# Two planned costs of a list-scheduled transformer kernel: the norm's application on GpSimd, and the engine of the first layer's key copies

## The chip, the cores and the metric

One core of a Trainium2 chip runs the whole program. The time is device microseconds for one execution, from launch to end. The kernel before the change was timed three times: 2121.66, 2126.34 and 2129.11 us, so the median is 2126.34 us. The engines are named as in the profile: PE is the matrix engine, PEld its weight loads, DVE the vector engine, ACT the scalar engine, POOL is GpSimd and SP the engine that only issues transfers.

## What is computed

Four transformer layers run over 16 sequences of 256 rows with 128 features. Each layer is a norm and an attention, then a norm and a feed-forward block, each added to the running `x`. All of it is 32-bit floating point.

```python
x = x + _L0_attn_ref(_layernorm(x), gamma, w_q, w_kv, null_kv, q_scale, k_scale, w_out)
x = x + _L0_ffn_ref(_layernorm(x), w1, b1, w2, b2)
x = x + _L1_attn_ref(...); x = x + _L1_ffn_ref(...)
x = x + _L2_attn_ref(...); x = x + _L2_ffn_ref(...)      # eight experts, the best one per row
x = x + _L3_attn_ref(...); x = x + _L3_ffn_ref(...)

def _layernorm(x, eps=1e-05):
    m = jnp.mean(x, -1, keepdims=True); v = jnp.var(x, -1, keepdims=True)
    return (x - m) / jnp.sqrt(v + eps)

# layer 0 attention, 16 heads of 64
q = _l2norm(q) * q_scale
k = _l2norm(k) * k_scale
sim = einsum('bhid,bhjd->bhij', q, k) * 8.0 + dist * slopes      # causal, two null keys
out = softmax(sim) @ v @ w_out
```

## The kernel before

**An order written by a planner.** The kernel does not issue instructions where its code stands. Each piece of work is a call `step(eng, p, ns, emit, r, w, m)`: the engine, a rank `p` that says how early the step is wanted, a planned length `ns`, a function that issues the instructions, and the tiles that it reads, writes or changes. When all steps are known, `Plan.run` goes through an imagined time line. Each engine has a time from which it is free; a step is ready when the steps it depends on have ended, plus a fixed delay for a signal to be seen (`SEEN`, for example 60 ns on DVE and 110 ns on POOL). Among the steps that an engine could start within 40 ns of its earliest, the one with the lowest rank is taken. Then the engine whose pick starts earliest goes first, its `emit` is called, and its free time moves on by the planned length. The result is a fixed order of instructions in each engine's queue. On the chip each queue runs strictly in that order, and waits where a tile isn't ready. So a planned length never delays an instruction by itself: it only decides which order, which engine and which buffer the steps get.

**Steps with two engines.** `"AD"` stands for ACT or DVE, `"DP"` for DVE or POOL, with one planned length for each. Such a step stands in both engines' lists and goes to the one that can start it first in the plan; the planned end breaks ties. A step of the kind `"AD"` counts on DVE with its rank raised by 8 (`SHY`), so DVE takes it only where it has nothing more urgent.

**The norm** (`layernorm`, line 456) is three steps: `stats` on DVE (four instructions, lines 464 and 465), `scale` on POOL (variance plus epsilon, line 469 or 471, and the power −½, line 436), and `apply`, two instructions of 128x128 in line 477 that subtract the mean and multiply. In the first layer `apply` is called with `eng="DVE"`; in all later places (attention and feed-forward of layer 1, attention and expert gate of layer 2, attention and feed-forward of layer 3) with the default `"DP"`, 96 norms in all. The step before the change is planned with 520 ns on DVE and 620 ns on POOL. What reads its result is the turn (transposition) in PE, line 432, by way of `turned` and `in_halves`.

**The first layer's preparation** (`prep0`, line 787) projects `xn` to raw queries and keys (line 404), copies them out of the accumulation banks (`evac`, lines 448 on ACT and 450 on DVE), squares and sums them (lines 812 and 813), takes the power −½ on POOL (line 436, planned with 2892 ns), and in `scaled` (line 821) multiplies the raw values in place on DVE (line 827), turns them on PE (line 432) into two banks, one for each half, and copies each half into `Q` or `K`. The two copies of a query turn are `evac` steps, free to go to ACT or DVE. The two copies of a key turn, line 843, also multiply by a per-partition scale `kqs` and are fixed to ACT, planned with 570 ns. There are 32 key turns and so 64 such copies, 128x512 each. The scores' matmuls (line 404, tiles `K` and `Q`) read them, then line 866 (DVE) and line 874 (ACT) make the softmax's numerators, and line 534 (POOL) divides.

**Banks.** All matrix results go through eight accumulation banks, `t0x` to `t7x`; a bank is free again when its last copy has been made. In the first layer each queue holds work of two or three sequences at once, since the preparation of a sequence runs up to 26 ranks ahead of its scores and a sequence takes 16 ranks.

The parts that set which engine gets a step, in `Plan.run`:

```python
could.append((t, s.p + (self.SHY if e == "DVE" and s.eng[0] == "ACT" else 0), s.no, s))
...
t, p, _, s = min((c for c in could if c[0] <= soon + 40), key=lambda c: c[1:3])
pick = (t, t + s.ns[e] if len(s.eng) > 1 else t, p, e, s)
if best is None or pick[:3] < best[:3]:
    best = pick
```

Of the kernel before, what the change touches and what calls it, by code (L numbers as in the profile page):

```python
# [11 lines left out]
AF = mybir.ActivationFunctionType  # L12
ALU = mybir.AluOpType
# [54 lines left out]
class Plan:  # L68
# [27 lines left out]
    def step(self, eng, p, ns, emit, r=(), w=(), m=(), mode=None, tail=None):  # L96
        s = Step()
        s.eng = {"AD": ("ACT", "DVE"), "DP": ("DVE", "POOL")}.get(eng, (eng,))
        s.ns = dict(zip(s.eng, ns)) if len(s.eng) > 1 else {eng: ns}
        s.p, s.emit, s.mode, s.tail, s.no = p, emit, mode, tail, len(self.steps)  # L100
        val = lambda x: x if isinstance(x, Value) else self.key(x)
        r, w, m = ([val(x) for x in xs] for xs in (r, w, m))
        deps = {}
        for v in r:
            deps.update((id(d), d) for d in v.writers)
        for v in w:
            deps.update((id(d), d) for d in v.readers)
        for v in m:
            deps.update((id(d), d) for d in v.writers + v.readers)
        for v in r:  # L110
            v.readers.append(s)
        for v in w:
            v.writers.append(s)
        for v in m:
            v.writers, v.readers = [s], []
        s.touch = list({id(v): v for v in r + w + m if v.home}.values())
        for v in s.touch:
            v.steps += 1

        for src in r:  # L120
            if src.home in self.BANKS:
                for made in src.writers:
                    for v in w:
                        if v.home and v not in made.touch:
                            made.touch.append(v)
                            v.steps += 1
        deps.pop(id(s), None)
        s.deps, s.left, s.users, s.end = list(deps.values()), len(deps), [], None
        for d in s.deps:
            d.users.append(s)  # L130
        self.steps.append(s)
        return s
# [107 lines left out]
def preln_d4_kernel(ctx: ExitStack, tc: tile.TileContext, x_in, vecs, rows, nullk, nullv,  # L240
                    wa0, wlat, wb1, wa2, wex, gatew, wa3, out):
    nc = tc.nc
    PSUM = bass.MemoryType.PSUM
    plan = Plan()
    step, get = plan.step, plan.get
# [195 lines left out]
    X = [plan.key(f"x{b}") for b in range(B)]  # L441
# [14 lines left out]
    def layernorm(b, p, xn, at, times=1, behind=(), eng="DP"):  # L456

        ln, x = get("ln"), x_of(b)  # L460

        def stats(e):
            for i in range(2):
                nc.vector.bn_stats(ln.t[0][:, i, :], x[:, i, :])
                nc.vector.bn_aggr(ln.t[1][:, i, :], ln.t[0][:, i, :])  # L465

        def scale(e):
            if times == 1:
                nc.gpsimd.tensor_scalar(ln.t[2], ln.t[1][:, :, 1], LN_EPS, 1.0, ALU.add, ALU.mult)  # L469
            else:  # L470
                nc.gpsimd.tensor_scalar(ln.t[2], ln.t[1][:, :, 1], 1.0 + LN_EPS, LN_EPS * LN_EPS, ALU.mult, ALU.add)
            rsqrt(ln.t[2], 2)

        def apply(e):
            for i in range(2):
                v = nc.vector if e == "DVE" else nc.gpsimd
                v.tensor_scalar(xn.t[:, (at + i) * D:(at + i + 1) * D], x[:, i, :], ln.t[1][:, i, 0:1],
                                ln.t[2][:, i:i + 1], ALU.subtract, ALU.mult)

        step("DVE", p, 788, stats, r=[X[b]], w=[ln])  # L480
        step("POOL", p, 1070, scale, m=[ln])
        step(eng, p, (520, 620) if eng == "DP" else 520 if eng == "DVE" else 620, apply, r=[X[b], ln] + list(behind), w=[xn])

    def turned(p, xn, nt, gamma=None):

# [265 lines left out]
    kqs = cp.tile([P, 1], F32, tag="kqs", name="kqs")  # L751
# [12 lines left out]
    def null2(e):  # L764
# [7 lines left out]
         r=["nss"], w=[nk_ps], mode="P")  # L772
    step("DVE", -13, 100, lambda e: nc.vector.scalar_tensor_tensor(
        nkT, nk_ps.t[:, 0:16].rearrange("p (c n) -> p c n", n=2), kqs, steepT.unsqueeze(2).broadcast_to([P, 8, 2]), ALU.mult, ALU.mult),
         r=[nk_ps, "steepT"], w=["nkT"])
# [11 lines left out]
    def prep0(b):  # L787
        st = {}
        lo, hi = first[0, b - 1] if b else A0 - 16, first[0, b] - 2
        lo = max(lo, hi - LEAD0)  # L790
        order = ("x p00 p01 p20 p21 p10 p11 p30 t00 p31 t01 v0 v1 t10 v2 v3 t11").split()
        at = {what: lo + 2 + (hi - lo - 2) * i / len(order) for i, what in enumerate(order)}
        xn = get("r")
        layernorm(b, lo, xn, 0, times=2, eng="DVE")
        xnT = turned(at["x"], xn, 2, gamma=vec("gamma"))
        st.update(Q=[get("Q"), get("Q")], K=[get("K"), get("K")], V=[get("V"), get("V")], pn=get("pn"))
        for c in range(2):
            step("POOL", at["t10"] - 4, 180,
                 lambda e, c=c: nc.gpsimd.tensor_copy(st["K"][c].t[:, :, 0:2], nkT[:, 4 * c:4 * c + 4, :]),
                 r=["nkT"], w=[st["K"][c]])  # L800
        raws, ss = {}, [get("ss") for _ in range(4)]

        def project(n, c):

            i, which = divmod(n, 2)
            p = at[f"p{n}{c}"]
            ps, sq = get("t"), get("sq")
            raw = raws[n, c] = get("r")
            step("PE", p, 862, lambda e: mm(ps.t, xnT.t[:, i * P:(i + 1) * P], wqkv[:, (2 * which + c) * 512:(2 * which + c + 1) * 512]),
                 r=[xnT, f"wA.{2 * which + c}"], w=[ps], mode="P")  # L810
            evac(p, raw, ps, lambda: (raw.t, ps.t))
            step("ACT", p, 520, lambda e: nc.scalar.activation(sq.t, raw.t, AF.Square), r=[raw], w=[sq])
            step("DVE", p, 592, lambda e: nc.vector.tensor_reduce(ss[n].t[:, c * 8:(c + 1) * 8], sq.t.rearrange("p (h d) -> p h d", d=64),
                                                                  AX.X, ALU.add), r=[sq], w=[ss[n]])
            if c == 1:
                step("DVE", p, 80, lambda e: nc.vector.tensor_scalar(ss[n].t, ss[n].t, 1e-24, None, ALU.max), m=[ss[n]])  # L816
                step("POOL", p - 6, 2892, lambda e: rsqrt(ss[n].t, 16), m=[ss[n]])
                if which == 1:
                    step("DVE", p - 6, 80, lambda e: nc.vector.tensor_tensor(ss[n].t, ss[n].t, steep, ALU.mult), r=["steep"], m=[ss[n]])

        def scaled(which, c):

            p, t, of = at[f"t{which}{c}"], [get("t"), get("t")], [raws[which, c], raws[2 + which, c]]
            for i in range(2):
                n, raw = 2 * i + which, of[i]
                r = lambda raw=raw: raw.t.rearrange("p (h d) -> p h d", d=64)
                step("DVE", p - 2, 598, lambda e, n=n, r=r: nc.vector.tensor_tensor(
                    r(), r(), ss[n].t[:, c * 8:(c + 1) * 8].unsqueeze(2).broadcast_to([P, 8, 64]), ALU.mult), r=[ss[n]], m=[raw])

            def turn(e):  # L830
                for i in range(2):
                    for k in range(4):
                        turned_halves(t, i * 256 + k * 64, of[i].t[:, k * P:(k + 1) * P])

            step("PE", p, 500, turn, r=of, w=t, mode="S")
            for z in range(2):
                src = lambda z=z: t[z].t.rearrange("p (i c q) -> p c i q", i=2, c=4)
                dst = lambda z=z, x=st["KQ"[which == 0]][c], a=2 * which: x.t[:, :, a:a + 256].rearrange(
                    "p c (i z q) -> p c i z q", i=2, z=2)[:, :, :, z]
                if which == 0:  # L840
                    evac(p, st["Q"][c], t[z], lambda src=src, dst=dst: (dst(), src()))
                else:
                    step("ACT", p - 8, 570, lambda e, src=src, dst=dst: nc.scalar.activation(dst(), src(), AF.Copy, scale=kqs),
                         r=[t[z]], w=[st["K"][c]])

        def values(k):
            i, c = divmod(k, 2)
            ps, p = get("t"), at[f"v{k}"]
            step("PE", p, 862, lambda e: mm(ps.t, xnT.t[:, i * P:(i + 1) * P], wqkv[:, 2048 + c * 512:2048 + (c + 1) * 512]),
                 r=[xnT, f"wA.{4 + c}"], w=[ps], mode="P")  # L850
            evac(p, st["V"][i], ps, lambda: (st["V"][i].t[:, c * 512:(c + 1) * 512], ps.t))

        for n in (0, 2, 1, 3):
            for c in range(2):
                project(n, c)
        for which in range(2):
            for c in range(2):
                scaled(which, c)
        for k in range(4):
            values(k)  # L860
        return st
# [60 lines left out]
    for b in range(B):  # L922
        st = prep0(b)
# [139 lines left out]
    for b in range(B):  # L1063
        st = prep1(b)
# [302 lines left out]
    for b in range(B):  # L1367
        st = prep2(b)
# [123 lines left out]
    for b in range(B):  # L1492
        st = prep3(b)
# [95 lines left out]
```

## Time and profile before

| what | value |
|---|---|
| median of three runs | 2126.34 us |
| the profiled execution, whole / its span | 2132.18 us / 2130.5 us |
| granted clock of PE, mean | 0.982 |
| busy of the span: PE, PEld, DVE | 2030.3, 1395.8, 1636.7 us |
| busy of the span: ACT, POOL | 1660.5, 1159.3 us |
| line 843 on ACT, 128x512 | 64 instructions, 677 to 707 ns |
| line 477 on POOL, 128x128 | 134 instructions, 779 to 817 ns |
| line 477 on DVE, 128x128 | 122 instructions, 309 to 976 ns, median 342 ns |
| copies of 128x512 into `Q` (first layer) | 32 on ACT, median 612 ns; 32 on DVE, median 679 ns |

The span runs from the first to the last instruction; the whole time has 1.7 us more around it. The busy time of an engine is the union of its instructions; PE's is close to the span throughout, while the other three have between 470 and 971 us in which nothing runs. In time order the program does layer 0 up to some 577 us, layer 1 to about 1100 us, layer 2's attention to about 1740 us, with the experts and layer 3 mixed at the end.

The 64 key copies lie between 30.7 and 565.9 us. The norms that may go to either engine begin at about 577 us: 67 of the 96 went to POOL, 29 to DVE.

### The profile page before, as it was taken

How to read it: one execution, taken by the hardware profiler on the slowest of the kernel's cores; microseconds unless marked ns; L12 is line 12 of the kernel's file. 1: busy time of each engine (PE TensorE's matmuls, PEld its weight loads, DVE VectorE, ACT ScalarE, POOL GpSimd, SP SyncE). 2: the span in 40 equal slices, each digit the busy share in tenths (PEclk: the TensorE clock that was granted, in tenths of full speed). 3: DMA queues.
4: the chain of work that ended last, by engine and by line, in shares of the span. 5: the costliest groups of instructions: out<-in, count | busy, mean ns of one | idle time of the engine just before them, and what ended most of it. 6: DMA issues, size and time to landing. Idle time of an engine off the chain costs nothing.

```text
span 2130.5 us, 86226 instructions
## 1 busy us (share of the span) xinstructions
PE 2030.3 (95%) x34860; PEld 1395.8 (66%) x34860; DVE 1636.7 (77%) x6393; ACT 1660.5 (78%) x4834; POOL 1159.3 (54%) x2157
## 2 busy tenths in 40 slices
PE   7999999999999999999999999999999998998997
PEld 4667777777665444544546677777887775775665
DVE  7999999999887766667665467777676778677997
ACT  6999999998887776767766668877666778677996
POOL 7888888898842121212223346666454974227642
PEclk9999999999999999999999999999999998998999
DMA  5000000000140000000000000000442001441000
GB/s 168 2 2 2 2 2 2 2 2 3 32 61 12 2 3 3 3 3 3 3 3 1 2 4 5 7 7 18 123 122 74 22 7 45 140 146 29 15 8 18
DMA packets 60303, 59.08 MB, mean 28 GB/s; under 512 B 28016, under 2 KB 49024, under 8 KB 59904
## 3 DMA queue, kind: packets, MB, share of 16 engines
q1 hardware_dynamic: 57680, 49.33, 8.3%
q8 instruction: 274, 4.49, 0.9%
q0 software_dynamic: 2048, 4.20, 0.6%
q14 instruction: 125, 1.02, 0.2%
q10 hardware_dynamic: 176, 0.03, 0.0%
HBM read 43.32 MB, written 10.22 MB: 25 GB/s over the span
## 4 chain that ended last, share of the span: by engine, by line
PE 73%; DVE 12%; POOL 7%; ACT 6%; issue 3%; another core or an unknown queue 0%; POOLq 0%; ACTq 0%; DVEq 0%
PE t0x L404 9%; PE t4x L404 9%; PE t6x L404 8%; PE t1x L404 8%; PE t7x L404 8%; PE t3x L404 7%; PE t2x L404 7%; PE t5x L404 7%; PE t1x L432 1%; PE t5x L432 1%; PE t6x L432 1%; PE t7x L432 1%; PE t0x L432 1%; PE t4x L432 1%; PE t2x L432 1%
## 5 line engine op out<-in xcount | busy, mean ns | idle before, releaser
L469 POOL TENSOR_SCALAR ln_rs4x<-ln_mv4x 128x2 f32<-128x2 f32 x24 | 4.6, 193 | 92.1 <-DVE ln_mv4x L465 91.1
L469 POOL TENSOR_SCALAR ln_rs2x<-ln_mv2x 128x2 f32<-128x2 f32 x21 | 4.7, 224 | 82.7 <-DVE ln_mv2x L465 81.9
L469 POOL TENSOR_SCALAR ln_rs0x<-ln_mv0x 128x2 f32<-128x2 f32 x21 | 4.1, 193 | 78.1 <-DVE ln_mv0x L465 70.6
L469 POOL TENSOR_SCALAR ln_rs3x<-ln_mv3x 128x2 f32<-128x2 f32 x23 | 4.8, 210 | 70.9 <-DVE ln_mv3x L465 64.1
L502 POOL TENSOR_TENSOR x<-x,row_sb 128x256 f32<-128x256 f32 x48 | 35.0, 730 | 6.2 <-DVE row_sb L1118 3.4
L436 POOL TENSOR_TENSOR ss0x<-ss0x,mhalf 128x16 f32<-128x16 f32 x11 | 31.9, 2902 | 8.5 <-DVE ss0x L816 7.3
L469 POOL TENSOR_SCALAR ln_rs1x<-ln_mv1x 128x2 f32<-128x2 f32 x23 | 4.4, 193 | 57.0 <-DVE ln_mv1x L465 55.9
L534 POOL TENSOR_SCALAR probs4x<-probs4x,sums2x 128x256 f32<-128x256 f32 (+2 forms) x44 | 20.4, 477 | 25.3 <-PE t5x L404 16.5
L534 POOL TENSOR_SCALAR probs0x<-probs0x,sums2x 128x256 f32<-128x256 f32 (+2 forms) x40 | 19.2, 493 | 26.3 <-DVE sums2x L529 16.0
L534 POOL TENSOR_SCALAR probs0x<-probs0x,sums4x 128x256 f32<-128x256 f32 (+2 forms) x44 | 21.7, 506 | 21.2 <-DVE sums4x L529 20.9
L436 POOL TENSOR_TENSOR ss3x<-ss3x,mhalf 128x16 f32<-128x16 f32 x11 | 32.9, 2992 | 0.1
L436 POOL TENSOR_TENSOR ss1x<-ss1x,mhalf 128x16 f32<-128x16 f32 x11 | 32.8, 2986 | 0.1
L436 POOL TENSOR_TENSOR ss2x<-ss2x,mhalf 128x16 f32<-128x16 f32 x11 | 31.9, 2901 | 0.9 <-DVE sums1x L529 0.9
L436 POOL TENSOR_TENSOR ss5x<-ss5x,mhalf 128x16 f32<-128x16 f32 x10 | 30.5, 3045 | 0.2
L436 POOL TENSOR_TENSOR ss4x<-ss4x,mhalf 128x16 f32<-128x16 f32 x10 | 29.4, 2944 | 0.5 <-DVE sums1x L529 0.5
L1060 POOL TENSOR_TENSOR x<-x,sq0x 128x512 f32<-128x512 f32 x4 | 5.1, 1275 | 44.9 <-DVE sq0x L1058 44.9
L534 POOL TENSOR_SCALAR probs2x<-probs2x,sums0x 128x256 f32<-128x256 f32 (+2 forms) x44 | 19.7, 463 | 17.8 <-DVE sums1x L529 14.0
L534 POOL TENSOR_SCALAR probs2x<-probs2x,sums4x 128x256 f32<-128x256 f32 (+2 forms) x40 | 20.9, 535 | 12.3 <-DVE sums4x L529 11.9
L534 POOL TENSOR_SCALAR probs3x<-probs3x,sums3x 128x256 f32<-128x256 f32 (+2 forms) x44 | 19.8, 464 | 13.4 <-DVE sums3x L529 12.1
L621 DVE CUSTOM_DVE_ANT_0 probs2x<-t6x,mask 128x128 f32<-128x128 f32 (+1 forms) x44 | 11.9, 323 | 19.6 <-PE t2x L404 7.6
L534 POOL TENSOR_SCALAR probs5x<-probs5x,sums3x 128x256 f32<-128x256 f32 (+2 forms) x44 | 20.5, 482 | 11.9 <-DVE sums3x L529 11.8
L534 POOL TENSOR_SCALAR probs0x<-probs0x,sums0x 128x256 f32<-128x256 f32 (+2 forms) x44 | 21.7, 507 | 9.2 <-DVE sums1x L529 6.7
(5024 smaller groups left out, 10840.1 us busy)
## 6 DMA issues: line engine op xcount, KB each, us to landing
w0x<-in_wex_dram SPq DMA_DIRECT2D x16, 578.0 KB, 4.1
w1x<-in_wex_dram SPq DMA_DIRECT2D x15, 578.0 KB, 4.8
w2x<-in_wex_dram SPq DMA_DIRECT2D x15, 578.0 KB, 3.9
w_wA<-in_wa_dram SPq DMA_DIRECT2D x18, 256.0 KB, 4.6
ex_rows<-zero SPq DMA_DIRECT2D x2, 1472.0 KB, 29.2
w_wB<-in_wb_dram SPq DMA_DIRECT2D x11, 256.0 KB, 5.4
x<-in_x_dram SPq DMA_DIRECT2D x8, 256.0 KB, 6.2
ex_y<-bT1x SPq DMA_DIRECT2D x20, 64.0 KB, 3.4
```

Of the source, the lines that this page charges most:

```text
L404: nc.tensor.matmul(o[c], lhsT[:, c], rhs, start=start, stop=stop, **kw)
L432: nc.tensor.transpose(t[z].t[:, c:c + 64], block[r], ident[r, r])
L436: nc.gpsimd.tensor_tensor(t, t, mhalf[:t.shape[0]].broadcast_to([t.shape[0], n]), ALU.pow)
L469: nc.gpsimd.tensor_scalar(ln.t[2], ln.t[1][:, :, 1], LN_EPS, 1.0, ALU.add, ALU.mult)
L502: step("POOL", p, 670, lambda e: nc.gpsimd.tensor_tensor(x_of(b), x_of(b), row_over(name, 2), ALU.add), r=reads, m=[X[b]])
L534: nc.gpsimd.tensor_scalar(pr.t[:, j, a:z], pr.t[:, j, a:z], sums.t[:, i:i + 1], 1.0, ALU.mult, ALU.mult)
L621: nc.vector.tensor_tensor_reduce(pr.t[:, g % 2, c], s[g].t[:, c], m, -1.0, 3.0e38, ALU.add, ALU.min, nm.t[:, j:j + 1])
L1060: step("POOL", lo + 30, 1300, lambda e: nc.gpsimd.tensor_tensor(x, x, ys.t.rearrange("p (c d) -> p c d", d=D), ALU.add), r=[ys, "w1"], m=xx)
```

## The change

The planned length of a norm's application on POOL goes from 620 to 1640 ns. The key copies of the first layer become steps for ACT or DVE, planned with 570 and 610 ns; on DVE the copy is a `tensor_scalar` with the same per-partition scale, on ACT it stays the same activation.

```diff
-        step(eng, p, (520, 620) if eng == "DP" else 520 if eng == "DVE" else 620, apply, r=[X[b], ln] + list(behind), w=[xn])
+        step(eng, p, (520, 1640) if eng == "DP" else 520 if eng == "DVE" else 620, apply, r=[X[b], ln] + list(behind), w=[xn])
...
                 else:
-                    step("ACT", p - 8, 570, lambda e, src=src, dst=dst: nc.scalar.activation(dst(), src(), AF.Copy, scale=kqs),
-                         r=[t[z]], w=[st["K"][c]])
+                    def keyed(e, src=src, dst=dst):
+                        if e == "DVE":
+                            nc.vector.tensor_scalar(dst(), src(), kqs, None, ALU.mult)
+                        else:
+                            nc.scalar.activation(dst(), src(), AF.Copy, scale=kqs)
+
+                    step("AD", p - 8, (570, 610), keyed, r=[t[z]], w=[st["K"][c]])
```

No instruction is added or removed; no transfer, tile or weight is touched. Since every later choice of the planner follows from its time line, the order, the engines of two-engine steps and the buffer numbers may differ from the first key copy on.

## The prediction

> **What bounds the kernel now.** I read the page's busy rows first, then a table of busy time by stage, the waits of PE, ACT and DVE in the first layer, and the instructions of line 477.
>
> ```profile
> core 0: us, PE busy (x) PEld busy (x) DVE busy (x) ACT busy (x) POOL busy (x), PEclk, DMA share, GB/s
> 0.00:57.00 57.00, 43.01 (x404) 27.05 (x404) 42.38 (x148) 40.03 (x109) 42.66 (x90) 1.00 0.49 157
> 57.00:577.00 520.00, 509.42 (x7400) 367.60 (x7402) 485.65 (x1818) 475.97 (x1480) 459.64 (x886) 0.99 0.02 5
> 577.00:1100.00 523.00, 510.37 (x9808) 273.38 (x9808) 365.68 (x1659) 382.15 (x916) 122.14 (x185) 1.00 0.06 10
> 1100.00:1740.00 640.00, 627.94 (x8760) 479.57 (x8750) 434.62 (x1173) 457.10 (x1476) 355.49 (x707) 1.00 0.11 32
> 1740.00:2131.00 391.00, 339.59 (x8500) 248.15 (x8500) 308.33 (x1599) 305.22 (x856) 179.41 (x292) 0.92 0.19 55
> ```
>
> A row is a stretch in us, its length, then each engine's busy time. PE lacks 14.0 us in the start, 10.6 in the rest of layer 0 (520 − 509.4), 12.6 in layer 1, 12.1 in layer 2's attention and 51.4 in the last stretch. PE sets the pace up to 1740 us. In layer 0 the others are close behind: DVE idle 34.4 us of 520, ACT 44.0, POOL 60.4. Only in the last stretch is there much to win.
>
> ```profile
> PE t7x L432 <- DVE Q1x L450: 2.3, 1, 2.3
> PE t1x L432 <- DVE Q1x L450: 1.8, 1, 1.8
> PE t5x L432 <- DVE r0x L827: 1.8, 1, 1.8
> PE t5x L432 <- DVE r9x L827: 1.8, 2, 0.9
> ...
> ACT K1x L843 <- PE t1x L432: 6.1, 3, 3.2
> ACT K2x L843 <- PE t4x L432: 3.5, 2, 2.5
> ```
>
> These are waits of PE and of ACT between 57 and 577 us: total, times, longest. PE's own waits there are for DVE, at the scaling of line 827 and at banks that a query copy has yet to empty. ACT stands before key copies until PE has turned the keys; over all 64 copies its idle time there adds up to 27 us. Nobody on PE waits for line 843.
>
> The rule of Perfetto Trace Analysis in the Trainium skill (Identifying the Most-Contended Engine) speaks against my reading: it takes matmul busy time as a poor measure of PE's headroom and wants the weight loads' share. That is 367.6 of 520 us here, so by the rule some 152 us (an estimate) would be open to a better order in layer 0; by the gaps in PE's row it is 10.6. The run shows gaps, and I use those.
>
> **The key copies.** On ACT a copy takes 688 ns (677 to 707). No row shows the same on DVE, so I bound it: the query copy, same shape and same turn, takes 679 ns on DVE; a `tensor_scalar` with a per-partition scalar from a bank (line 1139, 128x256) takes 484 where the plain copy of 128x256 takes 425, so 679 + 59 = 738 ns at most. I take 700.
>
> ```profile
> L1139 DVE TENSOR_SCALAR Q0x<-t7x,vec_sb x8: 476/484/484, 1057.2 to 1699.0; 128x256 f32<-128x256 f32 x8
> L843 ACT ACTIVATE K1x<-t3x,kqs x5: 681/692/707, 32.4 to 414.9; 128x512 f32<-128x512 f32 x5
> ```
>
> How many move? The query copies, free in the same way, went 32 to 32; I take 32 of 64 (bounds 0 and 64). ACT loses 32 x 0.688 = 22.0 us, DVE gains 32 x 0.70 = 22.4 (21.7 to 23.6). The step issues one instruction and no transfer. The cover: I paired each two key copies with the next weight load that reads their `K`; in three of four pairs of the steady stretch the copies end 3.3 to 19.8 us before it, in the fourth 0.42 us, and PE is busy with other turns then. So shorter latency on the way to the scores gains nothing there. At the start it may: the copies of 30.7 and 31.3 us end 0.11 us before the first scores; side by side they would end 0.6 us sooner, but DVE's next piece, a sum of line 813, starts as much later. I take −0.5 us (0 to −0.6).
>
> DVE's load is the danger. Behind a key copy in DVE's queue stand line 827, the sums of line 813 that POOL's power waits for, and the score work of line 866; PE waits for the first and last of these. DVE would stand at 485.7 + 22.4 = 508.1 of 520 us. But about as many free copies go to DVE as to ACT already (164.1 and 164.4 us in lines 450 and 448), and the planner hands some back when DVE is late: a copy of 128x512 takes 681 to 691 ns on DVE and some 590 on ACT. With half handed back, DVE rises to 497. The closest row is the query copy: before its 32 on DVE, DVE sat idle 0.4 us in all. I take 0 for layer 0; bounds −10.6 (all of PE's idle time) and +23.6 (the whole load added to a DVE that keeps its present waits).
>
> The Trainium skill, Perfetto Trace Analysis, Optimizing Scalar/DVE Operations, advises taking work off a full DVE rather than giving it more, and states overheads of some 125 ns for DVE and 51 for ScalarE on PSUM. By those figures 32 moved copies would cost 2.4 us of engine time (an estimate), against 0.4 by my rows.
>
> **The norm's application.** Two instructions, no transfer, 2 x 797 ns and little between them: 1.6 us on POOL where the plan had 0.62. Their number stays.
>
> ```profile
> 1815.48 1.59 POOL L477 TENSOR_SCALAR r5x<-x,ln_mv1x,ln_rs1x 128x128 f32<-128x128 f32 x2
> 1817.06 1.57 POOL L477 TENSOR_SCALAR r5x<-x,ln_mv4x,ln_rs4x 128x128 f32<-128x128 f32 x2
> 1818.62 1.57 POOL L477 TENSOR_SCALAR r2x<-x,ln_mv0x,ln_rs0x 128x128 f32<-128x128 f32 x2
> 1820.27 0.72 POOL L502 TENSOR_TENSOR x<-x,row_sb 128x256 f32<-128x256 f32 x1
> ...
>   PEld t5x L432: 3.2, 1
> ```
>
> The first lines are POOL's queue, three norms in a row; the last is the longest wait for line 477 anywhere, at 2121 us, and it was for an application on DVE. I paired each of the 67 applications on POOL with the first turn that reads it: the turn comes 0.8 to 65 us later, median 34.7. So being 1 us later than planned costs nothing before, and planning it right repairs no visible wait. If that cover were gone, the 26 applications on POOL after 1740 us could cost 1.0 us each. Line 477 comes back to back on POOL 7 times; in the new plan the second of such a pair may find DVE free first. Seven moved norms put 7 x 0.69 = 4.8 us on DVE and take 11.2 from POOL; DVE is 79% busy after 1740 and 68% between 1100 and 1740, so 0 of it on the path, 4.8 as the bound. Behind an application on POOL stand the next norm's scale, the bias of line 502, layer 3's key masks (line 596, 1.9 us) and the gather and scatter transfers that POOL issues; these get planned places 1 us later. SP's queue sees no change but order.
>
> **The new order.** Everything after the first key copy is planned anew, so the order changes even where nothing else does. PE changes between tile shapes 654 times in this run, and each time the next matmul starts only about 70 ns before the last one ends; a 128x128 matmul lasts 272 ns and is followed after 58, so a change costs 272 − 70 − 58 = 144 ns. Five per cent more or fewer changes, 33, is ±4.7 us. In the last stretch I take a fifth of PE's 51.4 us of idle time as the bound either way, ±10, and −2.5 us (a twentieth) as the value, as POOL's planned time there comes nearer to the real one by some 26 us.
>
> **Sum.** −0.5 + 0 + 0 − 2.5 = −3.0 us. The profiled execution took 2132.18 us, 2130.5 of span and 1.7 around it; that is 5.8 us above the median of the runs shown. So 2132.2 − 3.0 = 2129.2 for such an execution, and 2126.3 − 3.0 = 2123.3 us, which I round to 2123, for the median. A difference under 0.3%, 6.4 us, can't be told from none.
>
> **The rivals.** *Faster*: the new order wins a quarter of the last stretch's 51.4 us of idle time (−12.9) and 2 us of layer 0's: 2126.3 − 14.9 = 2111. For it: PE's last stretch has the most gaps and its granted clock is only 0.92. Against it: no wait there is for a POOL application. *Slower by a full DVE*: a key copy waits on DVE for the turn as it does on ACT. Half of ACT's 27 us would be 13.6 us of forced standing; 485.7 + 22.4 + 13.6 = 521.7, and half of the old idle time, 17.2, stays as well: 538.9. Handing back 16 copies (−10.9) leaves 528.0 in a stretch of 520: +8.0, so 2134; without handing back 2145. It decides once DVE's work and forced standing pass 520 us in layer 0. Against it: DVE's copies of `Q`. *A worse order at the end*: +10 as bounded above, 2136. *The change does not do what it says*: DVE's rank handicap of 8 keeps all keys on ACT, and applications stay on POOL; then only small reordering, 2126.
>
> **Chances and range.** Forecast 0.36, no effect 0.05, faster 0.33, slower by DVE 0.16, slower at the end 0.10. So faster by over 0.3%: 0.33; within: 0.41; slower: 0.26. The forecast's own range is 2120 to 2132. To hold 8 in 10 it reaches over most of both sides: down to 2100 (−26: 10.6 of layer 0 and 15 after it), up to 2146 (DVE full with nothing handed back).
>
> **What would show it.** Right: line 843's successors about half on DVE at 680 to 740 ns; DVE near 497 us busy in layer 0; PE's idle time in 57 to 577 us still near 11 us; line 477 on POOL 55 to 67 times; the gain, if any, in the last stretch. Wrong: layer 0 ends more than 5 us from 577 us; PE waits for DVE at lines 827 or 450 that add to more than 20 us; shape changes far from 654; a turn that waits for line 477 on POOL.

## The result: slower by half a per cent, all of it before 750 us

The changed kernel takes 2135.97 us in the median of eight runs (2131.57 to 2140.89), the kernel before 2124.82 us in eight runs (2121.58 to 2129.11). The ratio is 1.0046, with a 95% interval of 1.0031 to 1.0062. The forecast was 2123 us: the sign was wrong.

The profiled executions hide it: 2132.7 us of span after, 2130.5 before. The profile of before happened to run at a lower granted clock in its last stretch (0.92 against 0.95), 7 us above its kernel's median. So the comparison goes by places in the program, not by the two spans. Line 497 adds a sequence's attention to `x`, 64 times in all, 16 in each layer; the times of these adds mark how far the program is.

| place | before, us | after, us | difference |
|---|---|---|---|
| 5th add of layer 0 | 230.6 | 232.4 | +1.8 |
| 13th add of layer 0 | 520.1 | 528.2 | +8.2 |
| last add of layer 0 | 613.7 | 619.6 | +5.9 |
| 9th add of layer 1 | 884.5 | 895.5 | +11.0 |
| 5th add of layer 2 | 1351.3 | 1362.2 | +10.9 |

Layer 0 loses 6 us, the hand-over to layer 1 another 5, and from there on both run at the same pace. Counting started matmuls says the same: the changed kernel starts its 8,500th (614 us before) 6.6 us later, its 10,000th (685 us) 10.8 us later, and from the 11,000th (745 us) on it stays 11.0 us behind. In the steady part of layer 0 two sequences (one pair, which the plan repeats) take 72.36 us before and 73.95 after.

First the busy time by stage of the changed kernel (columns as in the table of before):

```profile
core 0: us, PE busy (x) PEld busy (x) DVE busy (x) ACT busy (x) POOL busy (x), PEclk, DMA share, GB/s
0.00:57.00 57.00, 44.16 (x378) 27.05 (x380) 43.78 (x149) 37.56 (x99) 40.91 (x85) 0.96 0.49 157
57.00:577.00 520.00, 508.74 (x7344) 365.85 (x7342) 492.13 (x1798) 459.30 (x1455) 460.43 (x872) 1.00 0.02 5
577.00:1100.00 523.00, 508.91 (x9702) 275.08 (x9700) 367.41 (x1676) 380.15 (x912) 125.41 (x195) 0.99 0.06 9
1100.00:1740.00 640.00, 629.63 (x8783) 476.31 (x8781) 431.09 (x1163) 454.15 (x1475) 345.15 (x690) 1.00 0.10 32
1740.00:2133.00 393.00, 340.84 (x8668) 251.09 (x8664) 319.00 (x1629) 313.25 (x882) 188.96 (x315) 0.95 0.18 55
```

In the same 520 us PE is as busy as before (508.7 against 509.4) but has done 56 matmuls fewer. DVE is up by 6.5 us, ACT down by 16.7.

The waits of PE and ACT between 57 and 577 us in the changed kernel (total, times, longest):

```profile
PE t0x L432 <- DVE r8x L827: 1.5, 2, 1.0
PE t0x L432 <- DVE r6x L827: 1.0, 1, 1.0
...
PE t6x L432 <- DVE K1x L845: 0.8, 1, 0.8
...
ACT K0x L847 <- PE t2x L432: 6.8, 3, 3.2
ACT K2x L847 <- PE t2x L432: 6.1, 2, 3.0
```

These visible waits add up to little more than before (PE's idle time in the 520 us is 11.3 us against 10.6), and the longest are shorter. ACT still stands before its 32 key copies for 28 us in all, as it did before 64. What ACT was spared it did not turn into work. The key copies on DVE, and the rows of line 843's successor on ACT:

```profile
L845 DVE TENSOR_SCALAR K0x<-t1x,kqs x2: 748/750/751, 30.4 to 167.9; 128x512 f32<-128x512 f32 x2
L845 DVE TENSOR_SCALAR K2x<-t3x,kqs x2: 718/734/749, 62.0 to 422.5; 128x512 f32<-128x512 f32 x2
...
L847 ACT ACTIVATE K1x<-t7x,kqs x1: 690/690/690, 536.3 to 536.3; 128x512 f32<-128x512 f32 x1
```

32 of the 64 went to DVE, 718 to 751 ns each, median 745.5. The next instruction on DVE starts 664 ns later (on ACT 586), which is what a copy takes from its queue.

The chain that ended last, shares of the span by engine. The page of before:

```profile
PE 73%; DVE 12%; POOL 7%; ACT 6%; issue 3%; another core or an unknown queue 0%; POOLq 0%; ACTq 0%; DVEq 0%
```

The page of the changed kernel:

```profile
PE 67%; DVE 16%; POOL 8%; ACT 5%; issue 3%; POOLq 0%; ACTq 0%; DVEq 0%
```

Over the eight steady sequences the shift is larger: of each pair's time the chain has 51.6 us on PE, 17.6 on POOL and 2.1 on DVE before, and 33.5, 18.7 and 19.7 after. DVE has come into the chain that PE and POOL formed. That alone does not explain the loss: in f1 and n2 below, DVE has only 7.4 and 4.1 us of the chain, and their pairs (73.73 and 73.83 us) are nearly as slow as the changed kernel's (73.95).

### The profile page after: what moved, and what is told of

It reads as the page before. It is cut to its first block, busy times and chain, and to the rows that moved or that the text cites. A ratio compares the mean times of both kernels' runs of the same rounds, so it can differ in the third digit from the quotient of the medians.

```text
span 2132.7 us, 86213 instructions
## 1 busy us (share of the span) xinstructions
PE 2032.3 (95%) x34860; PEld 1395.4 (65%) x34860; DVE 1653.4 (78%) x6412; ACT 1644.4 (77%) x4817; POOL 1160.9 (54%) x2155
## 4 chain that ended last, share of the span: by engine, by line
PE 67%; DVE 16%; POOL 8%; ACT 5%; issue 3%; POOLq 0%; ACTq 0%; DVEq 0%
PE t2x L404 9%; PE t6x L404 8%; PE t1x L404 8%; PE t4x L404 7%; PE t3x L404 7%; PE t5x L404 7%; PE t0x L404 7%; PE t7x L404 6%; PE t3x L432 1%; PE t0x L432 1%; PE t6x L432 1%; PE t1x L432 1%; PE t7x L432 1%; PE t4x L432 1%; PE t5x L432 1%
## 5 line engine op out<-in xcount | busy, mean ns | idle before, releaser
L534 POOL TENSOR_SCALAR probs0x<-probs0x,sums2x 128x256 f32<-128x256 f32 (+2 forms) x40 | 18.7, 480 | 27.5 <-DVE sums2x L529 16.0
L534 POOL TENSOR_SCALAR probs2x<-probs2x,sums0x 128x256 f32<-128x256 f32 (+2 forms) x44 | 19.7, 461 | 17.3 <-DVE sums1x L529 14.9
L534 POOL TENSOR_SCALAR probs4x<-probs4x,sums4x 128x256 f32<-128x256 f32 (+2 forms) x44 | 22.6, 525 | 11.7 <-DVE sums4x L529 8.4
L534 POOL TENSOR_SCALAR probs2x<-probs2x,sums2x 128x256 f32<-128x256 f32 (+2 forms) x44 | 20.1, 470 | 12.3 <-DVE sums2x L529 9.7
```

The lines of the kernel that those rows point to most:

```text
L534: nc.gpsimd.tensor_scalar(pr.t[:, j, a:z], pr.t[:, j, a:z], sums.t[:, i:i + 1], 1.0, ALU.mult, ALU.mult)
```

## The experiments

Eleven more kernels were run; each ratio is to the kernel of before as timed on the same chip. The theories: **A**, the 32 copies on DVE overload it; **B**, the plan was drawn anew and this draw orders the work worse, whoever copies; **C**, the planned length of 1640 ns is at fault; **D**, DVE's copy is planned too short. "Pair" is the time of two steady sequences, a quarter of the way from the 5th to the 13th add. "Stalls" is worked out from the trace over the same stretch: for each two neighbouring matmuls of one tile shape, where the second starts within 70 ns of another engine's release, the distance above the usual one, summed and given per pair. Each pair time comes from one profiled execution. Kernels that share the order of layer 0 and its engines agree: 72.36 and 72.33 us (before and e2), 73.95 and 74.00 (after and e1).

| kernel | ratio to before (95%) | pair, us | stalls, us |
|---|---|---|---|
| before | 1 | 72.36 | 1.46 |
| after | 1.0046 (1.0031 to 1.0062) | 73.95 | 2.94 |
| e1 keys alone | 1.0061 (1.0045 to 1.0077) | 74.00 | 2.98 |
| e2 length alone | 0.9998 (0.9985 to 1.0010) | 72.33 | 1.50 |
| e3 new order, keys on ACT | 1.0079 (1.0064 to 1.0093) | 74.81 | 3.48 |
| e4 old order, 32 keys on DVE | 1.0077 (1.0062 to 1.0092) | 74.12 | 2.89 |
| n1 keys on ACT, planned 586 | 1.0050 (1.0033 to 1.0067) | 75.03 | 3.20 |
| n2 keys on ACT, planned 620 | 1.0018 (1.0002 to 1.0033) | 73.83 | 2.44 |
| n3 keys on ACT, planned 540 | 1.0088 (1.0071 to 1.0105) | 75.26 | 3.49 |
| r1 keys on ACT, later rank | 1.0004 (0.9990 to 1.0018) | 72.93 | 1.90 |
| d1 keys free, real prices | 1.0038 (1.0026 to 1.0050) | 74.42 | 3.31 |
| f1 new order, light keys | 1.0031 (1.0019 to 1.0042) | 73.73 | 2.54 |
| f2 old order, light keys | 1.0029 (1.0019 to 1.0039) | 72.71 | 1.81 |

**Which half of the change.** The keys alone:

```diff
-step(eng, p, (520, 1640) if eng == "DP" else ...
+step(eng, p, (520, 620) if eng == "DP" else ...
```

> The key copies free to go to ACT or DVE, the norm's application planned with 620 ns as before. Theory A (the 32 key copies on DVE cost layer 0 its 11 us): +0.4 to +0.6%, two sequences of layer 0 take 73.9 us as in the changed kernel. Theory C (the planned length of 1640 ns is at fault): within 0.2% of before, 72.4 us for two sequences. A result over +0.7% would say that the planned length wins something back.

And the length alone, on the kernel of before:

```diff
-step(eng, p, (520, 620) if eng == "DP" else ...
+step(eng, p, (520, 1640) if eng == "DP" else ...
```

> The application planned with 1640 ns, the key copies all on ACT. Theory A: within 0.2% of before, layer 0 at 72.4 us for two sequences, since no norm with two engines stands there. Theory C: +0.3 to +0.6%, lost after 577 us. The prediction's own term was -2.5 us (-0.1%), from the last stretch.

The keys bring the whole loss and the length none; C falls. The length moved only two norms off POOL (65 of 96 there, where it had been 67).

**Load or order.** The same order with the DVE copies handed to ACT, and the old order with half of the copies handed to DVE:

```diff
 def keyed(e, src=src, dst=dst):                       # e3, from the changed kernel
-    if e == "DVE":
-        nc.vector.tensor_scalar(dst(), src(), kqs, None, ALU.mult)
-    else:
-        nc.scalar.activation(dst(), src(), AF.Copy, scale=kqs)
+    nc.scalar.activation(dst(), src(), AF.Copy, scale=kqs)
...
-step("ACT", p - 8, 570, lambda e, ...: nc.scalar.activation(dst(), src(), AF.Copy, scale=kqs), ...)
+def keyed(e, src=src, dst=dst, z=z):                  # e4, from the kernel before
+    if z == 1:
+        nc.vector.tensor_scalar(dst(), src(), kqs, None, ALU.mult)
+    else:
+        nc.scalar.activation(dst(), src(), AF.Copy, scale=kqs)
+step("ACT", p - 8, 570, keyed, ...)
```

> The changed kernel's plan and order, but the 32 key copies that the plan gives to DVE are issued on ACT at the same point of the order. Theory A (load on DVE): DVE loses 23.8 us, ACT gains 22; two sequences of layer 0 come back to 72.4 us or less, the time to within 0.2% of before. Theory B (the new order is worse, whoever copies): it stays at 73.9 us and +0.4 to +0.6%, or gets slower still as ACT's queue was planned without these copies.

> The plan and order of before, but the second copy of each key turn is issued on DVE, 32 of 64. Theory A: DVE gets 23.8 us more with nothing handed back, so layer 0 loses at least what the change lost, 73.9 us or more for two sequences, +0.5 to +1.1%. Theory B: the old order keeps 72.4 us, within 0.2%.

Both are slower than the changed kernel. Here is the row for the eight steady sequences, first of the kernel before, then of e3 (stretch, length, busy PE, PEld, DVE, ACT, POOL):

```profile
230.63:520.06 289.43, 285.88 (x4194) 206.62 (x4192) 272.68 (x1014) 268.39 (x825) 256.59 (x497) 1.00 0.01 2
```

```profile
234.04:533.28 299.24, 293.09 (x4194) 210.09 (x4192) 273.62 (x1005) 268.60 (x834) 263.08 (x498) 1.00 0.01 2
```

In e3 DVE and ACT are as busy as before, to within 1 us of 289, for the same 4194 matmuls, and yet 9.8 us are lost: load on DVE is no explanation there. But e4 loses with the old order, so A is not dead either. Changing the order alone or the engine of the copies alone cost more here than changing both; that a queue's order and the engines of its copies fit each other is one reading of it.

**Other draws.** Five more kernels. n1, n2, n3 and r1 are edits of the kernel of before and keep every key copy on ACT; d1 is an edit of the changed one:

```diff
-step("ACT", p - 8, 570, lambda e, src=src, dst=dst: ...
+step("ACT", p - 8, 586, ...                           # n1; 620 in n2, 540 in n3
...
-step("AD", p - 8, (570, 610), keyed, ...
+step("AD", p - 8, (586, 664), keyed, ...              # d1
...
-step("ACT", p - 8, 570, lambda e, src=src, dst=dst: ...
+step("ACT", p - 4, 570, ...                           # r1
```

> The kernel of before, with one planned length altered: a key copy on ACT is planned with 586 ns (its measured distance to the next instruction) where it stood at 570. No engine changes for it. Theory A (keys on DVE cost the time): 72.3 to 72.6 us for two sequences of layer 0, within 0.2% of before. Theory B (the order of before is a lucky draw of the planner, and any other draw loses): 73 to 74.5 us and +0.2 to +0.7%.

> As the last, planned with 620 ns: a second new draw with every key copy on ACT. Theory A: 72.3 to 72.6 us, within 0.2%. Theory B: 73 to 74.5 us, +0.2 to +0.7%.

> A third new draw with all keys on ACT, planned with 540 ns. Theory A: 72.3 to 72.6 us for two sequences, within 0.2% of before. Theory B: 73 to 75 us, +0.2 to +0.7%, like the draws with 586 and 620.

> The changed kernel with the keys planned at the measured distances, 586 ns on ACT and 664 on DVE, where it had 570 and 610; the plan still gives 32 to DVE. Theory D (the change loses because DVE's copy is planned 54 ns too short): back to 72.4 us, within 0.2% of before. Theory A: 73.5 to 74.5 us, +0.3 to +0.7%, since the same 32 are on DVE. Theory B gives no sign either way, 72.4 to 74.5.

> The kernel of before, the key copies on ACT with a rank 4 later, so that ACT takes other ready work first: ACT's 27 us of standing before key copies should shrink. Theory A: 72.4 us or less, -0.2 to +0.1%. Theory B: it is one more draw, 73 to 74.5 us.

A new order alone can cost as much as the change did. A planned length altered by 16 ns, with every key copy on ACT as before, costs 0.50% (n1); by 30 ns the other way 0.88% (n3), nearly twice the change's loss. The rows of n2 and then n3 for their eight steady sequences, and that of the changed kernel last:

```profile
229.80:525.13 295.33, 291.68 (x4194) 209.58 (x4192) 273.73 (x1017) 268.69 (x821) 258.02 (x497) 1.00 0.01 2
```

```profile
235.80:536.84 301.04, 292.68 (x4188) 210.32 (x4186) 279.05 (x1014) 263.92 (x810) 256.36 (x493) 0.99 0.01 2
```

```profile
232.44:528.25 295.81, 290.45 (x4194) 208.78 (x4192) 282.22 (x1021) 259.54 (x818) 262.44 (x498) 1.00 0.01 2
```

n3 is 11.6 us longer than before, with no key on DVE. Other two-engine copies do change sides in such a draw, and n3's DVE is busy 6.4 us more than before, so n3 mixes order and load. n2 is the clean case: DVE and ACT are busy within 1.1 us of before, and these eight sequences still take 5.9 us more, nearly the 6.4 us of the changed kernel. The order of before is a good draw: of the four other draws with all keys on ACT one was level (r1) and three lost 0.18 to 0.88%. The two with keys on DVE, at either price, lie inside that spread; D falls with d1, where real prices left the pair at 74.42 us. One part of the change's loss these draws do not show: between the last add of layer 0 and the 9th of layer 1 they take 270.4 to 271.6 us, as before (270.8), while the orders planned with free keys take longer, as the next experiment tells. The expectation of r1 was met by A's number, but its pair rose by 0.6 us, and ACT's standing before key copies only fell from 27 to 22 us.

**A lighter DVE in both orders.** The copies on DVE take a quarter of the columns and leave the rest of those keys out. f1 has the order of the changed kernel; f2, with the order of before, gives DVE the second copy of each turn, as e4 does:

```diff
-    plan.home("K", many(sp, "K", 3, [4, 258]))
+    Ks = many(sp, "K", 3, [4, 258]); [nc.vector.memset(k, 0.0) for k in Ks]; plan.home("K", Ks)
...
-nc.vector.tensor_scalar(dst(), src(), kqs, None, ALU.mult)
+nc.vector.tensor_scalar(dst()[:, 0:1], src()[:, 0:1], kqs, None, ALU.mult)
```

> The changed kernel, queue by queue in the same order, but the 32 key copies on DVE take only a quarter of their columns (128 of 512; three clears of the key tiles stand at the program's start). This leaves three quarters of half of layer 0's keys unscaled and uncopied. DVE's 664 ns a copy falls to some 200, 14.8 us less in layer 0, and ACT stays relieved. Theory A (the load on DVE): two sequences of layer 0 take 72.4 us or less, the time is within 0.2% of before or below it. Theory B (the draw, the new order loses even with a lighter DVE): 73 to 74 us, +0.2 to +0.5%.

> The same light copies in the order of before: 32 key copies on DVE with a quarter of their columns, 32 whole ones on ACT (the same part of the keys left out). Both theories: below the 74.1 us of whole copies in this order. Theory A: 72.4 us or less, the same as with the new order. Theory B: 71 to 72.3 us, at least 0.7 us below the new order at equal load.

The steady rows, of f1 and then of f2:

```profile
231.32:526.24 294.92, 290.81 (x4194) 208.56 (x4192) 276.77 (x1022) 259.94 (x818) 262.56 (x498) 1.00 0.01 2
```

```profile
232.95:523.77 290.82, 287.18 (x4194) 206.91 (x4192) 276.03 (x1029) 261.96 (x809) 255.81 (x497) 1.00 0.01 2
```

The light copies saved less than expected: one still filled 335 ns of DVE's queue in f1 and 263 in f2, against 664 for a whole one and the 200 foreseen. At equal load on DVE (276.8 and 276.0 us) the new order needs 4.1 us more for these eight sequences. In the steady part, then, the order carries most of the loss: lightening DVE brings the new order's pair down by 0.22 us only, of 1.60. The whole time is less clear. f1 and f2 end level (1.0031 and 1.0029), since f2 loses 1.6 us more before the 5th add and ends layer 0 more slowly, while the new order loses at the hand-over to layer 1 whatever the keys weigh: between the last add of layer 0 and the 9th of layer 1 lie 275.9 us after the change and 274.3 to 274.9 in f1, e1, e3 and d1, against 270.8 before and 272.3 in f2. The changed kernel and f1, e1, e3 and d1 are the ones whose plan has the free key step, in two orders of layer 0 (d1 has its own); why they lose there was not found. How the whole 11 us divide between load, order and this hand-over stays open. No version was faster than the kernel before; the length alone and the later rank were level.

## Where the time goes inside PE's busy row

The two kernels' matmuls are the same, and so are the changes of tile shape: 18 in a pair and 5.1 us in them, before and after. Yet a pair's busy time on PE rose from 71.47 to 72.61 us and its idle time from 0.89 to 1.34 (a quarter of the rows above). Most of the loss is thus in PE's busy row. One case in the changed kernel, the same in each pair, in the timeline, first DVE, then POOL, then PE (start, length, engine, line, tiles; in brackets the idle time before it):

```profile
367.96 0.88 DVE L827 TENSOR_TENSOR r13x<-r13x,ss5x 128x512 f32<-128x512 f32 x1
368.76 0.17 DVE L816 TENSOR_SCALAR ss0x<-ss0x 128x16 f32<-128x16 f32 x1
368.84 0.28 DVE L871 CUSTOM_DVE_ANT_0 probs3x<-t4x,dist 128x130 f32<-128x130 f32 x1
...
369.05 0.42 DVE L871 CUSTOM_DVE_ANT_0 probs3x<-t4x,dist 128x258 f32<-128x258 f32 x1
...
368.25 0.64 POOL L799 COPY K0x<-nkT 128x8 f32<-128x8 f32 x1
...
368.88 0.22 PE L432 MATMUL t0x<-ident,pn0x 64*128 64x64 f32 x1
368.88 0.22 PE L432 MATMUL t3x<-ident,pn0x 64*128 64x64 f32 x1
369.05 0.27 PE L432 MATMUL t2x<-ident,probs0x 64*128 64x64 f32 x1
369.53 0.27 PE L432 MATMUL t4x<-ident,probs0x 64*128 64x64 f32 x1 [0.20 <-DVE nm11x L871]
```

Read it from below. The turn into bank `t4x` must wait until DVE has read that bank for the last time (line 871). The two matmuls of a turn usually start together, as into `t0x` and `t3x` just before; here the second starts 0.48 us after the first. The idle column shows 0.20 us, because the first counts as busy for 0.27. DVE was late partly since the scaling of line 827, usually 0.68 us, met a copy of POOL and took 0.88. Summed by the rule given above, such stalls are 1.46 us in a pair before and 2.94 after; of the latter DVE ends 2.67, 1.16 of it at the scaling of line 827 and 0.95 at banks that line 871 has yet to read. Their growth, 1.48, is close to the pair's growth of 1.60, and over the thirteen kernels stalls and pair rise together: below 2 us of stalls all pairs are below 73 us, above 2.4 all are above 73.7. The level depends on what is taken as usual: with the median distance of each two matmul forms the stalls are 2.6 us before and 4.0 after, and other choices put the growth between 0.9 and 2.1 us. That the stalls are the loss is thus supported by this agreement; no run removed them one by one.

The prediction had set aside the rule of the Trainium skill, Perfetto Trace Analysis, Identifying the Most-Contended Engine, that matmul busy time does not show how near PE is to its limit. The traces bear it out on this point: the idle time of PE moved by 0.45 us in a pair while the pair moved by 1.60. They don't show the 152 us that I had worked out from the weight loads' share.

## Why the prediction was wrong

- **The step that failed: "I take 0 for layer 0".** It measured +1.6 us a pair, 8.2 us at the 13th add. Two reasons. I bounded layer 0 by PE's gaps and waits and by DVE's load, and so by quantities that this profile shows only in part. And I let the new order act only in the last stretch ("I take a fifth of PE's 51.4 us of idle time"), though the order is new from the first key copy on and layer 0 is where four engines are each over 88% busy. By n1 to n3 a new order with every key on ACT puts a pair of layer 0 at 73.8 to 75.3 us. Of the signs named beforehand, layer 0's end came 5.9 us late, while PE's idle time (11.3 us) and its waits for lines 827 and 450 (6.6 us, where more than 20 was the sign) gave none.
- **The place of the loss** in the sum was therefore missed twice: layer 0 (+6) and its hand-over to layer 1 (+5), where the text read PE's pace up to 1740 us as fixed and saw much to win only after it.
- **The slower rival came near in time (2134) by the wrong mechanism.** It said that DVE would stand before a key copy until the turn is done. DVE stood there 0.17 us over 32 copies. The argument against it, from the query copies, was right; it only refuted this mechanism, not the loss.
- **Right: 32 of 64 copies move**, and the planner hands others back: my count was 16 of 128x512, worth 10.9 us; between 57 and 577 us the trace has 19 fewer of 128x384 and 10 fewer of 128x128 on DVE and 5 more of 128x512, 10.6 us less in all. DVE stands at 492 us of 520, against my 497.
- **DVE's price** was off: 700 taken, 738 as the bound, 745.5 measured. By the distance to the next instruction, the measure that fills a queue, it is 664 against 586 on ACT. d1 shows that this price did not decide.
- **The norm's length: right, at nothing.** e2 is level at 0.9998. 66 norms stay on POOL after the change, and no turn waits for one. The −2.5 us can't be told from none.
- **Shape changes** were the wrong reason for the order's effect: 18 a pair in each of these two kernels, 5.1 us in both.

## What to carry to other kernels

Where a list scheduler keeps several queues nine tenths full, the present order can be a lucky or a selected draw, and any edit of a planned cost draws again: measure a few harmless alterations first, and weigh the edit against their spread (here −0.0 to +0.9%). Giving a step a second engine was no gain here: ACT had 16.7 us less to do in layer 0 and stood before its key copies as long as before. And a loss of 1% in a busy matmul queue need not appear as idle time: compare distances between starts.

## What the runs showed of the hardware

Line 827 on DVE (two inputs in SBUF) and the small copy of line 799 on POOL slow each other where they overlap. The copy's rows of before, over 231 to 521 us (shortest, median, longest in ns):

```profile
L799 POOL COPY K2x<-nkT x6: 185/192/637, 243.3 to 508.9; 128x8 f32<-128x8 f32 x6
L799 POOL COPY K0x<-nkT x5: 186/193/639, 260.7 to 477.7; 128x8 f32<-128x8 f32 x5
```

And of the changed kernel, over 232 to 528 us:

```profile
L799 POOL COPY K2x<-nkT x6: 189/414/639, 244.3 to 516.4; 128x8 f32<-128x8 f32 x6
L799 POOL COPY K0x<-nkT x5: 183/637/642, 259.1 to 481.1; 128x8 f32<-128x8 f32 x5
```

In both kernels every copy that overlaps line 827 takes about 640 ns and every other about 190: 4 of 16 before, 8 of 16 after; line 827 itself goes from some 680 to between 797 and 899 ns with it. The Trainium skill, SBUF — State Buffer, Who interferes with whom, states that a DVE instruction with two SBUF inputs contends with a GpSimd instruction that reads SBUF; the runs agree. The new order had more of such meetings, but the pair times do not follow them (e4 has as few as before, d1 has none of them, and both are slow, at 74.12 and 74.42 us), so they are a part of some stalls and not the cause of the loss.
